# Three adjacency aggregations as 64x64 quadrant products in a four-layer graph network

## Chip, cores and metric

The kernel runs on one core of a Trainium2 chip. The metric is the device time of one execution in microseconds (us). With one core there is no second die to compare with. Engines are named as in the profile: PE is TensorE's matmuls, PEld its weight loads, DVE is VectorE, ACT ScalarE, POOL GpSimd, SP SyncE.

## The reference, cut to what matters

The input x has 128 batches of 64 tokens and 256 channels, in f32. Four layers follow, each `x + layer(relu(layernorm(x)))`. Three products with a 64x64 adjacency matrix concern us:

```python
# layer 0 (A_hat is adj with self loops, normalised by degrees)
agg = jnp.einsum('nm,bmd->bnd', A_hat, features)
h = jax.nn.relu(_batchnorm(agg.reshape(-1, d) @ W1.T + b1, g1, be1))   # statistics over all tokens
...
# layer 1
h = jax.nn.relu(jnp.einsum('ts,bsh->bth', adj, x @ Wg0 + bg0))
h = jax.nn.relu(jnp.einsum('ts,bsh->bth', adj, h @ Wg1 + bg1))
# ... then four small LSTMs over windows of h, which are most of the time
```

Layers 2 and 3 are attentions and are not touched.

## The kernel before

The 8192 tokens are worked on in 16 chunks of 512: four blocks (j) of 128 tokens, each of two batches. An aggregation multiplies each block by a 128x128 matrix with the adjacency twice on its diagonal, so half of each product is with zeros. Channels come in two halves k, and each half has a PSUM bank.

```python
def aggregate(src, mat, name):
    banks = []
    for k in range(KD):                       # KD = 2 channel halves
        ps = bank(f"agg{k}_{name}")           # one of eight PSUM banks, taken in turn
        for j in range(NJ):                   # NJ = 4 blocks of two batches
            nc.tensor.matmul(ps[:, j * P : (j + 1) * P], src[:, j, k * P : (k + 1) * P], mat,
                             start=True, stop=True)
        banks.append(ps)
    return banks
```

Layer 0's first pass, for each chunk c:

```python
xt = l0.tile([P, NJ, D], F32, tag="xt", bufs=3)
nc.sync.dma_start(xt, xr[c])
layernorm_relu(h, xt, f"a{c}")     # bn_stats on DVE, power on POOL, then nmr on DVE, then ACT
agg = l0.tile([P, KD, CH], F32, tag="agg", name=f"agg_{c}")
for k, ps in enumerate(aggregate(h, ahat_t, f"a{c}")):
    nc.vector.tensor_copy(agg[:, k, :], ps)                     # "the copies"
...
for m in range(KH):                                             # 4 output blocks of 128
    ps = bank(f"z1_{c}_{m}")
    for k in range(KD):
        nc.tensor.matmul(ps, w1_sb[:, k, m * P : (m + 1) * P], agg[:, k, :],
                         start=(k == 0), stop=(k == KD - 1))
    nc.scalar.activation(z1[c][m], ps, AF.Identity, bias=bn1_sb[:, 0, m : m + 1])
    nc.vector.bn_stats(st1[:, m, c, :], z1[c][m])               # "the statistics"
```

Within layernorm_relu `rstd` comes from GpSimd:

```python
rsqrt(rstd, mv[:, :, 1], EPS)                        # two POOL instructions
nc.vector.scalar_tensor_tensor(nmr, mv[:, :, 0], -1.0, rstd, op0=OP.mult, op1=OP.mult)   # "nmr"
```

In layer 1, PE's order is written by hand, and the aggregations stand as filler between LSTM steps. In layer 0 no order is written.

## Time and profile before

| What | Value | From |
|---|---|---|
| time | 2206.02 us median of 3 (2201.57 to 2208.31) | timed runs |
| layer 0, first pass: from one chunk's first z product to the next's, from the third chunk on | 9.23 to 9.36 us | PE in order of time |
| start of layer 0's second pass | 177.50 us | the same |
| LSTM stretch, from the first gate product to the last residual transposes | 346.91 to 1747.51, 1400.60 us | the same |
| one aggregation of one chunk in that stretch | 1.78 us | the same, quoted in the prediction |

The last column of such PE lines, in brackets, is idle time just before the group and what ended it; a group's time is best taken from its start to the next group's start, because the ends of pipelined matmuls overlap. The prediction below shows the lines that carry this. DVE in layer 0, in the order in which its instructions were issued (start, duration, line, names):

```profile
127.13 0.66 DVE L237 BATCH_NORM_STATS2 st<-z1b 128x6 f32<-128x512 f32 x1
127.71 1.27 DVE L227 COPY agg<-agg_a 128x512 f32<-128x512 f32 x2
128.90 0.16 DVE L149 SCALAR_TENSOR_TENSOR nmr_a<-mv_a,rstd_a 128x4 f32<-128x4 f32 x1
```

The order is: the last statistics of the previous chunk, the two copies, and then nmr, which belongs to the layernorm of a chunk further on. (Over the whole pass nmr waits 5.0 us for POOL, in four instances.)

### The profile page before, as it was taken

The page shows a single profiled execution, that of the slowest core. Times are in us where ns is not written, and L with a number is a line of the kernel's source. Part 1 is how long each engine was busy: PE and PEld are TensorE (multiplying, and loading weights), DVE is VectorE, ACT ScalarE, POOL GpSimd, SP SyncE. Part 2 cuts the span into 40 slices and gives each one's busy share as a digit, 9 for nine tenths or more (in the row PEclk, how much of TensorE's full clock was granted, in tenths as well). Part 3 has the DMA queues.
Part 4 walks back from the last instruction along what each step waited for, and adds up shares of the span by engine and source line. Part 5 has one row for each costly group of instructions (what it writes and reads, how often), then busy time and mean ns, then how long its engine had stood idle before and what let it go on. Part 6 is the DMA issues. An engine that isn't in the chain of part 4 may idle for free.

```text
span 2205.7 us, 24595 instructions
## 1 busy us (share of the span) xinstructions
PE 2101.8 (95%) x10117; PEld 1339.7 (61%) x10117; DVE 852.5 (39%) x1848; ACT 792.1 (36%) x1433; POOL 168.8 (8%) x216
## 2 busy tenths in 40 slices
PE   6999959999999999999999999999999899999996
PEld 3553435576577468468567657656746756666664
DVE  5643433223323322332332322323222256666664
ACT  3544413233333233333333422333333344444442
POOL 2100010001000000000100100000000011112211
PEclk9999969999999999999999999999999999999998
DMA  3100050000000000000000000000000100000000
GB/s 97 58 20 0 0 186 10 10 1 10 2 9 1 10 10 1 10 10 1 10 10 1 10 10 1 0 0 1 1 0 1 34 11 21 20 21 21 21 20 29
DMA packets 30127, 37.88 MB, mean 17 GB/s; under 512 B 1856, under 2 KB 27456, under 8 KB 30016
## 3 DMA queue, kind: packets, MB, share of 16 engines
q1 hardware_dynamic: 27600, 27.89, 4.1%
q0 software_dynamic: 2256, 8.40, 1.0%
q8 instruction: 79, 1.29, 0.2%
q14 instruction: 32, 0.26, 0.0%
q10 hardware_dynamic: 160, 0.03, 0.0%
HBM read 27.93 MB, written 8.39 MB: 16 GB/s over the span
## 4 chain that ended last, share of the span: by engine, by line
PE 77%; issue 10%; DVE 7%; POOL 3%; DMA 2%; ACT 1%; SPq 0%; POOLq 0%; DVEq 0%; ACTq 0%
PE g L369 32%; PE g L376 17%; PE z L250 5%; PE z L234 3%; PE p_q L500 3%; PE u L340 3%; PE p_k L500 2%; PE v L328 2%; DMA xt<-in_x_dram 2%; PE agg_b L161 1%; PE agg_c L161 1%; PE tr L523 1%; DVE s L514 1%; PE o L643 1%; PE o L588 1%
## 5 line engine op out<-in xcount | busy, mean ns | idle before, releaser
L369 PE MATMUL g<-hT,wih 128*128 128x256 f32 (+2 forms) x2496 | 826.7, 483 | 3.6 <-DVE hT L400 2.7
L369 PEld LDWEIGHTS g<-hT,wih 128*128 128x128 f32 x2496 | 465.0, 188 | 313.1 <-issue 182.4
L382 ACT ACTIVATE gate<-g,bias 128x256 f32<-128x256 f32 (+2 forms) x624 | 350.4, 562 | 820.0 <-PE g L376 648.1
L376 PE MATMUL g<-hs,whh 128*128 128x256 f32 (+2 forms) x1536 | 435.8, 437 | 0.0
L376 PEld LDWEIGHTS g<-hs,whh 128*128 128x128 f32 x1536 | 291.3, 190 | 132.2 <-issue 62.0
L386 DVE TENSOR_TENSOR cell<-cell,gate 128x256 f32<-128x256 f32 (+2 forms) x96 | 48.7, 507 | 449.7 <-ACT gate L382 449.7
L391 DVE TENSOR_TENSOR cell<-gate,gate 128x512 f32<-128x512 f32 (+2 forms) x80 | 48.2, 602 | 213.1 <-ACT gate L382 213.1
L234 PE MATMUL z<-agg,w_sb 128*128 128x512 f32 x256 | 117.5, 613 | 8.6 <-DVE agg L227 7.2
L250 PE MATMUL z<-h,w_sb 128*128 128x512 f32 x256 | 112.1, 601 | 5.0 <-ACT h L245 5.0
L392 ACT ACTIVATE gate<-cell 128x256 f32<-128x256 f32 (+2 forms) x176 | 89.8, 510 | 50.7 <-DVE cell L391 40.3
L410 POOL COPY hn<-hT 128x512 f32<-128x512 f32 x32 | 35.9, 1197 | 784.8 <-DVE hT L400 784.8
L400 DVE TENSOR_TENSOR hT<-gate,gate 128x512 f32<-128x512 f32 (+2 forms) x80 | 48.0, 600 | 114.0 <-PE g L369 96.9
L250 PEld LDWEIGHTS z<-h,w_sb 128*128 128x128 f32 x256 | 49.4, 193 | 67.7 <-issue 57.5
L234 PEld LDWEIGHTS z<-agg,w_sb 128*128 128x128 f32 x256 | 48.6, 195 | 67.4 <-issue 49.0
L395 DVE TENSOR_TENSOR hs<-gate,gate 128x256 f32<-128x256 f32 (+2 forms) x96 | 47.7, 497 | 69.8 <-ACT gate L392 49.6
L385 DVE TENSOR_TENSOR gate<-gate,gate 128x256 f32<-128x256 f32 (+2 forms) x96 | 47.7, 497 | 55.8 <-ACT gate L382 55.8
L508 POOL TENSOR_TENSOR s<-s,mx 128x256 f32<-128x256 f32 (+1 forms) x32 | 40.3, 1259 | 340.3 <-DVE mx L507 251.8
L495 ACT COPY v<-v 128x512 f32<-128x512 f32 x64 | 37.0, 578 | 76.6 <-PE v L492 76.6
L500 PE MATMUL p_q<-hT,w_sb 128*128 128x512 f32 x128 | 61.9, 606 | 0.3 <-DVE hT L175 0.3
L500 PE MATMUL p_k<-hT,w_sb 128*128 128x512 f32 x128 | 60.1, 592 | 0.0
L492 PE MATMUL v<-w_sb,hT 128*128 128x256 f32 x256 | 59.5, 386 | 0.0
L151 ACT ACTIVATE h<-xs,nmr_b,rstd_b 128x256 f32<-128x256 f32 x64 | 34.5, 590 | 69.6 <-DVE nmr_b L149 69.6
(153 smaller groups left out, 2068.1 us busy)
## 6 DMA issues: line engine op xcount, KB each, us to landing
xt<-in_x_dram SPq DMA_DIRECT2D x32, 512.0 KB, 3.8
out_dram<-o SPq DMA_DIRECT2D x16, 512.0 KB, 2.9
wih<-in_wih_t_dram POOLq DMA_DIRECT2D x4, 1024.0 KB, 13.4
whh<-in_whh_t_dram POOLq DMA_DIRECT2D x3, 1024.0 KB, 18.2
w_sb<-in_w_dram SPq DMA_DIRECT2D x1, 768.0 KB, 4.2
wqkv_sb<-in_wqkv_dram SPq DMA_DIRECT2D x1, 768.0 KB, 4.5
w_sb<-in_w1t_dram POOLq DMA_DIRECT2D x1, 512.0 KB, 4.9
w_sb<-in_w2t_dram POOLq DMA_DIRECT2D x1, 512.0 KB, 5.8
```

The lines of the kernel that those rows point to most:

```text
L234: nc.tensor.matmul(ps, w1_sb[:, k, m * P : (m + 1) * P], agg[:, k, :], start=(k == 0), stop=(k == KD - 1))
L250: nc.tensor.matmul(ps, w2_sb[:, k, m * P : (m + 1) * P], h1[:, k, :], start=(k == 0), stop=(k == KH - 1))
L340: nc.tensor.matmul(ps[:, i, :], v[:, k, j * P : (j + 1) * P], wg1_sb[:, k, :], start=(k == 0), stop=(k == KD - 1))
L369: nc.tensor.matmul(banks[q][:, :n].rearrange("p (j w e) -> p j w e", w=nw, e=2), wi[:, k, o], hv[:, k, :, cols, :], start=(k == 0), stop=( ...
L376: nc.tensor.matmul(banks[q][:, :n], wh[:, k, o], hs[:, k, :n], start=False, stop=(k == KD - 1))
L382: nc.scalar.activation(g[q], banks[q][:, :n], AF.Tanh if q == 2 else AF.Sigmoid, bias=bs[:, q * KD + c : q * KD + c + 1])
L386: nc.vector.tensor_mul(cell[c], cell[c], g[1])
L391: nc.vector.tensor_mul(cell[c], g[0], g[2])
L392: nc.scalar.activation(g[2], cell[c], AF.Tanh)
L400: nc.vector.tensor_mul(hv[:, c, :, cols, :], o.rearrange("p (j w e) -> p j w e", w=nw, e=2), t.rearrange("p (j w e) -> p j w e", w=nw, e=2))
L492: nc.tensor.matmul(ps[:, i, :], hT[:, k, j * P : (j + 1) * P], w[:, k, first : first + D], start=(k == 0), stop=(k == KD - 1))
L500: nc.tensor.matmul(ps, w[:, k, m * P : (m + 1) * P], hT[:, k, :], start=(k == 0), stop=(k == KD - 1))
```

## The change

The intent: work only with the two nonzero 64x64 blocks. A product of one batch and 64 channels needs a quarter of the array, and four such products were to run side by side (the prediction reads from layer 3's products that they do), so the aggregation should take less of PE's time.

```diff
 def aggregate(src, mat, name):
-    banks = []
+    banks = [bank(f"agg{e}_{name}").rearrange("p (k j t) -> p k j t", j=NJ, t=T) for e in range(2)]
     for k in range(KD):
-        ps = bank(f"agg{k}_{name}")
         for j in range(NJ):
-            nc.tensor.matmul(ps[:, j * P : (j + 1) * P], src[:, j, k * P : (k + 1) * P], mat,
-                             start=True, stop=True)
-        banks.append(ps)
-    return banks
+            for i in range(2):
+                for e in range(2):
+                    f = slice(k * P + i * T, k * P + (i + 1) * T)
+                    nc.tensor.matmul(banks[e][half(i), k, j, :], src[half(e), j, f],
+                                     mat[half(e), half(e)], start=True, stop=True)
+    return [ps.rearrange("p k j t -> p (k j) t") for ps in banks]
 # layer 0, and alike in layer 1's first aggregation
-for k, ps in enumerate(aggregate(h, ahat_t, f"a{c}")):
-    nc.vector.tensor_copy(agg[:, k, :], ps)
+for e, ps in enumerate(aggregate(h, ahat_t, f"a{c}")):
+    nc.vector.tensor_copy(agg.rearrange("p k (j e t) -> p e (k j) t", e=2, t=T)[:, e], ps)
 # layer 1's second: the interleaved matrix adjt_il goes, ScalarE's ReLU interleaves instead
-for k, ps in enumerate(aggregate(u, adjt_il, f"c{c}")):
-    nc.scalar.activation(hT[:, k, :], ps, AF.Relu)
+for e, ps in enumerate(aggregate(u, adjt_bd, f"c{c}")):
+    nc.scalar.activation(hT.rearrange("p k (n e) -> p e k n", e=2)[:, e],
+                         ps.rearrange("p (k j) t -> p k (j t)", k=KD), AF.Relu)
```

Besides the products, the banks change their meaning: one bank for each parity e of the batch, with both channel halves in it.

More of the change, by code (lines that the diff above doesn't have):

```diff
@@ L152, in layernorm_relu, with half @@
                                  scale=rstd[:, j : j + 1])
+    def half(r):
+        return slice(r * T, (r + 1) * T)
     def aggregate(src, mat, name):
-        banks = []
+        banks = [bank(f"agg{e}_{name}").rearrange("p (k j t) -> p k j t", j=NJ, t=T) for e in range(2)]
         for k in range(KD):
-            ps = bank(f"agg{k}_{name}")
             for j in range(NJ):
-                nc.tensor.matmul(ps[:, j * P : (j + 1) * P], src[:, j, k * P : (k + 1) * P], mat,
-                                 start=True, stop=True)
-            banks.append(ps)
-        return banks
+                for i in range(2):
[4 more added lines that the diff above has]
+        return [ps.rearrange("p k j t -> p (k j) t") for ps in banks]
     def to_channels(dst, src, name):
@@ L225 @@
             agg = l0.tile([P, KD, CH], F32, tag="agg", name=f"agg_{c}")
-            for k, ps in enumerate(aggregate(h, ahat_t, f"a{c}")):
-                nc.vector.tensor_copy(agg[:, k, :], ps)
+            for e, ps in enumerate(aggregate(h, ahat_t, f"a{c}")):
+                nc.vector.tensor_copy(
+                    agg.rearrange("p k (j e t) -> p e (k j) t", e=2, t=T)[:, e], ps)
             lo = res.tile([P, KD, CH], F32, tag=f"r{c}", name=f"z1a_{c}")
@@ L287 @@
         nc.vector.tensor_add(bias, bias, bias2)
-        adjt_il = w1.tile([P, P], F32, name="adjt_il")
-        nc.vector.tensor_copy(adjt_il.rearrange("p (t e) -> p e t", e=2),
-                              adjt_bd.rearrange("p (e t) -> p e t", e=2))
         wih_sb, whh_sb = [], []
@@ L320, in convolutions @@
             agg = l1.tile([P, KD, CH], F32, tag="g", name=f"agg1_{c}", bufs=3)
-            for k, ps in enumerate(aggregate(h, adjt_bd, f"b{c}")):
-                nc.vector.tensor_copy(agg[:, k, :], ps)
+            for e, ps in enumerate(aggregate(h, adjt_bd, f"b{c}")):
+                nc.vector.tensor_copy(
+                    agg.rearrange("p k (j e t) -> p e (k j) t", e=2, t=T)[:, e], ps)
             yield
@@ L535, in columns @@
             return slice(b * T, (b + 1) * T)
-        def half(r):
-            return slice(r * T, (r + 1) * T)
         def pairs(a, r):
```

## The prediction

> **What bounds the kernel now.** I read the page's first line and engine row, then the PE rows by shape, then the table of stretches, then single stretches in order of time.
>
> ```profile
> span 2205.7 us, 24595 instructions
> PE 2101.8 (95%) x10117; PEld 1339.7 (61%) x10117; DVE 852.5 (39%) x1848; ACT 792.1 (36%) x1433; POOL 168.8 (8%) x216
> ...
> L161 PE MATMUL agg_b<-adjt_bd,h 128*128 128x128 f32 x256 | 33.4, 287 | 14.4 <-ACT h L151 14.4
> L161 PE MATMUL agg_a<-ahat_t,h 128*128 128x128 f32 x256 | 33.0, 284 | 1.9 <-ACT h L151 1.9
> L161 PE MATMUL agg_c<-adjt_il,u 128*128 128x128 f32 x256 | 31.0, 275 | 0.0
> ```
>
> TensorE is busy 95% of the span; no other engine passes 39%. The three aggregations hold 97.4 us of it, 4.4%: that is all the change can touch. Each has 16 chunks x 8 products = 128 products and 256 records, so one f32 product is two records, and an aggregation of one chunk is 16 records. Busy is not the same as worth, so I ask in which stretch they lie (columns: window, its length, PE and weight-load busy, clock, DMA share, GB/s; these instructions alone).
>
> ```profile
> 20.00:177.00 157.00, 29.21 (x240) 29.16 (x240) 0.98 0.14 43
> 296.00:347.00 51.00, 9.80 (x64) 9.67 (x64) 0.68 0.48 178
> 347.00:524.00 177.00, 7.86 (x65) 7.76 (x64) 1.00 0.02 6
> 524.00:1590.00 1066.00, 46.70 (x384) 46.57 (x384) 1.00 0.02 5
> ```
>
> So 16 of the 48 blocks lie in layer 0's first pass (up to 177 us), four at the start of layer 1, and 28 inside the LSTM stretch from 347 to 1590 us. In that stretch the same view without the filter shows PE busy 1242.7 of 1243 us: time taken from PE there is time off the kernel. In layer 0 it is otherwise (PE first, then DVE, of one chunk):
>
> ```profile
> 135.41 1.95 PE L161 MATMUL agg_a<-ahat_t,h 128*128 128x128 f32 x16
> 137.67 7.13 PE L234 MATMUL z<-agg,w_sb 128*128 128x512 f32 x16 [0.31 <-DVE agg L227]
> ...
> 136.33 0.69 DVE L237 BATCH_NORM_STATS2 st<-z1b 128x6 f32<-128x512 f32 x1 [1.02 <-ACT z1b L236]
> 136.94 1.27 DVE L227 COPY agg<-agg_a 128x512 f32<-128x512 f32 x2
> ```
>
> The copies out of the aggregation start at 136.94, when DVE is done with the statistics of the previous chunk's last z, which itself waited for ScalarE's evacuation. The first bank was full about 0.9 us after 135.41. So z waits for a chain z, ScalarE, statistics, copy; PE's aggregation lies beside that chain. The reader should see that z began 0.05 us after the first copy (136.94 + 0.68), not after both.
>
> **What the Trainium skill says.** "TensorE: Matmul & The Clock Gate", section "LDWEIGHTS (loading the stationary operand)": loading costs columns / 1.2 ns, whatever the rows. Halving the columns would give 53 in place of 107 ns. The trace's load records are 192 ns for 128 columns and 135 ns for 64: they include latency, so the direction agrees and the formula isn't separately visible. Same page, "Part 3: Packing small matmuls — row/col tiling": matmuls in different row and column groups run concurrently. The trace agrees: 64 records of layer 3's 64x64 products take 1.04 to 1.09 us, 16 to 17 ns each, though each record lasts 218 ns. "TensorEngine Tiling (Array Packing)", "Key Properties": changing the tiling mode drains the engine. The trace shows a small cost, worked out below. Same page, "Gotcha 1: PSUM Pressure": different row tiles have to write different banks. This is why the new banks are one per batch parity e and no longer one per half k of the channels, and that is where I expect the loss.
>
> **The change part by part.** First, PE's work. A block before is 16 records of 128 columns. In the LSTM stretch it costs, from its start to the next group's start, 735.81 - 734.03 = 1.78 us and 776.25 - 774.47 = 1.78 us.
>
> ```profile
> 734.03 1.95 PE L161 MATMUL agg_b<-adjt_bd,h 128*128 128x128 f32 x16
> 735.81 7.37 PE L369 MATMUL g<-hT,wih 128*128 128x512 f32 x16
> ```
>
> A block after is 2 x 4 x 2 x 2 = 32 products, 64 records, of the very shape that layer 3 already has (64-row, 64-column stationary, 64 moving columns, column half outside, row half inside):
>
> ```profile
> 1917.12 1.04 PE L173 MATMUL tc_f<-ident,h 128*128 128x128 f32 x8
> 1918.09 1.16 PE L643 MATMUL o<-v,att 64*64 64x64 f32 x64
> 1919.18 1.98 PE L500 MATMUL p_q<-hT,w_sb 128*128 128x512 f32 x4
> 1921.00 1.88 PE L500 MATMUL p_k<-hT,w_sb 128*128 128x512 f32 x4
> 1922.72 1.88 PE L500 MATMUL p_q<-hT,w_sb 128*128 128x512 f32 x4
> ```
>
> The block itself takes 1.09 us. Going in: the eight transposes before it take 0.97 us to the next start, where eight before an ordinary product take 0.88 (544.77 to 545.65), so 0.09. Coming out: four 512-column records take 1.82, the next four 1.72, so 0.10. Sum 1.28 us, a saving of 0.50 a block. In the LSTM stretch nothing hides it: 28 x 0.50 = 14 us. The arithmetic is a quarter as much, but the time falls only by 28%, because per-record issue and the two changes of mode remain.
>
> Second, the evacuations. Their number and elements stay (two of 512 elements for each block). DVE's writes become runs of 64 elements with gaps; its hT product (L400) writes runs of two elements with gaps and takes 688 ns for 512, against 693 for a plain one (L391), so no dearer. ScalarE's ReLU now writes every second element; no row before shows such a write, and at 36% ScalarE has room even if 598 ns grew. In the LSTM stretch other work lies between the aggregation and its reader (agg_b at 556.76, its v at 572.62), so the new order of copies costs nothing.
>
> Third, in layer 0 nothing lies between. All products now fill both banks to the end of the block, and each bank holds one parity of both channel halves. z's first product needs channel half 0, hence both copies. The block ends about 1.3 us after its start, still before DVE is free (1.53 us after), so copies start where they did, and z starts after the second, 138.21 + 0.05 = 138.26, in place of 137.67: 0.59 later. Given back: today z's second weights wait for the second copy; z's 16 records take 6.97 us where 16 x 0.43 = 6.88 would do, so 0.09. Net loss 0.50 a chunk on 15 chunks (the first z waits for its weights' DMA), 7.5 us. Chunks with a late input load are 0.1 us longer today through two more statistics ahead of DVE's last one; the earlier end of the aggregation frees their buffer sooner, perhaps 0.5 us in all. Loss 7.
>
> Fourth, layer 1's start, two agg_b and two agg_c back to back: agg_b runs from 323.59 to 329.56 at half clock. It is paced by ScalarE until h is complete at about 327; after that half a block and the first v remain, so v might start at 328.1, 1.4 us earlier. agg_c runs 343.34 to 346.91; afterwards the LSTM waits for both ReLUs of the first chunk, to about 345.9, 1.0 earlier. An estimate of 2.4 us. The removed interleaved matrix is one small DVE copy, off the path.
>
> Sum: -14 - 2.4 + 7 = -9.4 us, so 2206.0 - 9.4 = 2196.6, about 2197 us.
>
> **The rivals.** (1) PE is the bound everywhere, so 48 x 0.50 = 24 us come off, 2182 us. For it: 95% busy. Against it: the layer-0 rows above, where the copy ends the wait. It could come about in part if DVE's instructions were ordered anew, with the copies ahead of the last statistics. (2) Changing the mode costs more beside the LSTM's products than in layer 3, or the fourfold number of PE records outruns instruction issue: 0.5 us more a block eats the gain, and with layer 0's loss the kernel becomes 2213. Against it: layer 3 sustains 64 records in 1.09 us amid such changes. (3) The LSTM's recurrence appears as a new wait once the filler is shorter. Against it: after agg_b the next step begins with 16 input products (4.8 to 7.2 us) before it needs hs; agg_c comes after a first-step half whose successor needs no hs. This would cost under 3 us. (4) Bank pressure: two banks at once instead of one after the other. The waits view has no PE wait for the LSTM's banks beyond 0.5 us in total, so I expect nothing.
>
> **Range and chances.** The LSTM part could be 10 to 19 us, layer 0's loss 0 to 9, the start 0 to 4; repeated runs spread from 2201.6 to 2208.3. Not all extremes meet: 2186 to 2205. Faster by over 2% would need 44 us, nearly half of all aggregation time, which a block of 1.28 in place of 1.78 can't give: 0.02. Slower by over 2% would need a mode change near a microsecond: 0.02. Within 2%: 0.96.
>
> **What would show it.** Each aggregation's PE row with 1024 records and 17 to 20 us busy, mean near 220 ns. In the LSTM stretch 1.2 to 1.35 us from an agg block's start to the next group's, and that stretch 14 us shorter. In layer 0 PE's idle time before z for DVE's copies up from 7.2 us to 20 to 26, and a period from z to z up from 9.23 to about 9.7 us. The prediction is wrong if that period is unchanged (DVE reordered), if the block costs 1.7 us or more, or if ScalarE's ReLU grows so much that gates wait for it.

## The result, and the profile after

The changed kernel took 2214.47 us (median of 4, 2213.3 to 2217.57), the kernel before 2206.61 us in its 4 runs. The ratio is 1.0042, with a 95% interval of 1.0022 to 1.0061. All ratios here are the mean time of one kernel's runs over the mean of the other's in the same rounds, so not quite the ratio of the quoted medians. It is within 2%, but slower, by 8 us, where 9 us less was forecast, and outside the range of 2186 to 2205.

First the page of the changed kernel: span, engines, and the aggregations' rows (count, then busy us and mean ns).

```profile
span 2215.7 us, 29204 instructions
PE 2081.9 (94%) x12421; PEld 1301.6 (59%) x12421; DVE 850.8 (38%) x1847; ACT 790.0 (36%) x1433; POOL 168.3 (8%) x216
...
L167 PE MATMUL agg_b<-adjt_bd,h 64*64 64x64 f32 x1024 | 21.0, 233 | 14.7 <-ACT h L151 14.7
L167 PE MATMUL agg_a<-ahat_t,h 64*64 64x64 f32 x1024 | 19.4, 227 | 1.9 <-ACT h L151 1.9
L167 PE MATMUL agg_c<-adjt_bd,u 64*64 64x64 f32 x1024 | 18.4, 221 | 0.0
```

PE was relieved as planned: the aggregations' busy time fell from 97.4 to 58.8 us, and PE's whole busy time by 20 us. Yet the span grew by 10. Such a pair says that PE waits somewhere that it did not. First the place where the gain should be, the LSTM stretch:

```profile
565.23 11.28 PE L373 MATMUL g<-hT,wih 128*128 128x512 f32 x24
576.43 1.16 PE L167 MATMUL agg_b<-adjt_bd,h 64*64 64x64 f32 x64
577.52 7.47 PE L373 MATMUL g<-hT,wih 128*128 128x512 f32 x16
584.83 7.03 PE L380 MATMUL g<-hs,whh 128*128 128x512 f32 x16
```

The block takes 577.52 - 576.43 = 1.09 us. The group ahead of it takes 11.20 where it took 11.11 before (545.65 to 556.76), and the one behind 7.31 where it took 7.20 (558.55 to 565.75). So 1.09 + 0.09 + 0.11 = 1.29 us for the block, against a forecast of 1.28. The whole stretch (368.23 to 1755.07) is 1386.84 us, 13.76 shorter. The gain is there.

The loss is in layer 0. PE's z products of some chunks, in order of time, and the two rows of the table of waits (total us, times, longest) that grew:

```profile
70.21 7.14 PE L240 MATMUL z<-agg,w_sb 128*128 128x512 f32 x16 [2.34 <-DVE agg L232]
...
80.78 7.13 PE L240 MATMUL z<-agg,w_sb 128*128 128x512 f32 x16 [2.34 <-DVE agg L232]
...
92.14 8.83 PE L240 MATMUL z<-agg,w_sb 128*128 128x512 f32 x16 [3.14 <-DVE agg L232]
...
158.19 7.13 PE L240 MATMUL z<-agg,w_sb 128*128 128x512 f32 x16 [1.60 <-DVE agg L232]
...
168.02 7.13 PE L240 MATMUL z<-agg,w_sb 128*128 128x512 f32 x16 [1.60 <-DVE agg L232]
```

```profile
PE z L240 <- DVE agg L232: 35.6, 15, 5.0
...
DVE nmr_a L149 <- POOL rstd_a L81: 20.6, 14, 1.5
```

The second pass starts at 199.80 in place of 177.50 us: 22.3 us lost, where 7 were forecast. The last four intervals are 9.83 us, 0.60 above the 9.23 of before; the forecast was about 9.7. The eleven before them are 10.56 us or longer. And nmr now waits 20.6 us for POOL, where the same row of before has 5.0. The chain of waits shows it in its place (start, us, what):

```profile
76.47 0.61 DVE st L243
77.08 0.16 DVE mv_a L145 x2
77.28 0.11 issue
77.39 0.24 POOL rstd_a L80
77.62 0.07 issue
77.70 1.05 POOL rstd_a L81
78.77 0.16 DVE nmr_a L149
78.93 0.60 DVE st L243
79.53 1.20 DVE agg L232 x2
80.78 7.15 PE z L240 x16
```

Read from below: z waited for both copies, the copies stood behind the last statistics, these stood behind nmr, and nmr waited for POOL's power. No data go from nmr to these statistics or copies; nmr is for a later chunk. It merely stands ahead of them in DVE's order, which the compiler had changed. The Trainium skill's "PSUM — Partial Sum Buffer", section "Engine vs sequencer instructions", says that VectorE's queue is strictly first in, first out; this trace agrees, as DVE sat idle for 1.54 us ahead of nmr (77.23 to 78.77) while the statistics' input was ready from 78.07 (ScalarE, 77.38 + 0.69).

The last four intervals have no such wait because no layernorm is left to prepare. They therefore separate the terms: 0.60 us a chunk for the second copy, 10.57 - 9.83 = 0.74 us for the wait. In two further chunks z itself ran 8.83 in place of 7.13 us. In the first the granted clock over 92.14 to 100.90 is 0.81 (0.50 from 92.71 to 96.12), after PE had idled 3.14 us; in the other it is 0.81 too, after 2.34 us. I call these z products at half clock, though the clock is halved for only a part of them.

What is left of the 10 us in the spans: from the second pass's start to layer 1's first aggregation another 1.0 us went (the shift grows from 22.3 to 23.3); layer 1's start, from agg_b to the first gate product, is 1.95 us shorter (23.32 to 21.37; forecast 2.4). The part after the LSTMs, which the change does not touch, is 460.6 in place of 458.2 us in these two profiles; in the other profiles it lies between 456.8 and 461, and I draw nothing from it: one and the same kernel has 456.8 in the eighth run and 460.7 in the tenth. The four profiles without quadrants in layer 1 all have 458.1 to 458.2; why the others scatter is not known.

### The profile page after: what moved, and what is told of

It is laid out like the page before. It is cut to its first block, busy times and chain, and to the rows that moved or that the text cites. A ratio compares the mean times of both kernels' runs of the same rounds, so it can differ in the third digit from the quotient of the medians. Undisturbed runs are those within 1.5% of the kernel's fastest.

```text
span 2215.7 us, 29204 instructions
## 1 busy us (share of the span) xinstructions
PE 2081.9 (94%) x12421; PEld 1301.6 (59%) x12421; DVE 850.8 (38%) x1847; ACT 790.0 (36%) x1433; POOL 168.3 (8%) x216
## 4 chain that ended last, share of the span: by engine, by line
PE 76%; issue 10%; DVE 8%; POOL 3%; DMA 2%; ACT 1%; SPq 0%; POOLq 0%; DVEq 0%; ACTq 0%
PE g L373 32%; PE g L380 17%; PE z L256 5%; PE z L240 4%; PE p_q L504 3%; PE v L331 2%; PE u L343 2%; PE p_k L504 2%; DMA xt<-in_x_dram 2%; PE tr L527 1%; DVE st L243 1%; PE agg_b L167 1%; PE o L644 1%; DVE s L518 1%; PE o L589 1%
## 5 line engine op out<-in xcount | busy, mean ns | idle before, releaser
L240 PE MATMUL z<-agg,w_sb 128*128 128x512 f32 x256 | 122.5, 634 | 37.8 <-DVE agg L232 35.6
```

## The experiments

**Theory A**: the quadrants do what was forecast; layer 0 loses because of the banks. z needs both copies, and the compiled order of DVE puts a wait for POOL ahead of them. **Rival B**: quadrant products amid full-array products delay layer 0 by themselves. Later rivals stand with their runs. An overview (medians in us; "period" is from z to z from the third chunk on, "pass 2" the start of layer 0's second pass, "LSTM" the length of that stretch, all from the profiles):

| Kernel | us | ratio to before | period | pass 2 | LSTM |
|---|---|---|---|---|---|
| before | 2205 to 2207 | 1 | 9.23 to 9.36 | 177.50 | 1400.60 |
| changed | 2214.47 | 1.0042 | 10.56 to 12.27, last four 9.83 | 199.80 | 1386.84 |
| 1 changed, order mended | 2198.25 | 0.9972 | 9.83 | 185.72 | 1386.83 |
| 2 quadrants in layer 1 only | 2191.14 | 0.993 | 9.23 to 9.33 | 175.69 | 1386.83 |
| 3 quadrants in layer 0 only | 2230.98 | 1.0116 | 10.56 to 12.26, last four 9.83 | 199.45 | 1400.58 |
| 4 before, banks alone changed | 2230.82 | 1.0117 | 10.88 to 12.57, last four 9.85 | 199.51 | 1400.59 |
| 5 as 2, copies first | 2188.9 | 0.993 | 8.80 to 9.23 | 171.98 | 1386.84 |
| 6 as 1, copies first | 2198.3 | 0.9969 | 9.62 | 182.23 | 1386.83 |
| 7 as 1, four banks | 2194.92 | 0.9955 | 9.36 | 178.59 | 1386.84 |
| 8 as 7, copies first | 2186.23 | 0.9909 | 8.68 to 8.88 | 167.78 | 1386.83 |
| 9 before, order alone changed | 2220.77 | 1.0068 | 10.49 to 12.19, last three 9.23 | 194.61 | 1400.58 |

The LSTM column alone says that layer 1's part is settled: 13.76 us wherever the quadrants are in layer 1, nothing where they are not.

**1. The changed kernel with DVE's order mended.** One edge of order for each chunk, no wait, no other work:

```diff
-nc.vector.scalar_tensor_tensor(nmr, mv[:, :, 0], -1.0, rstd, op0=OP.mult, op1=OP.mult)
+with tc.issue_after(behind) if behind is not None else nullcontext():   # behind: the second copy of chunk c-4
+    nc.vector.scalar_tensor_tensor(nmr, mv[:, :, 0], -1.0, rstd, op0=OP.mult, op1=OP.mult)
```

> The changed kernel, with one order edge for each chunk of layer 0: VectorE's small product for a later chunk's layernorm (which waits for GpSimd's power) is issued behind the two copies out of the aggregation, as in the kernel before, where the changed kernel issues it ahead of the last statistics and the copies. Theory A (the lost 22 us of layer 0 are the second copy, 0.60 us a chunk, plus this wait, 0.74 us a chunk and more in the first chunks, plus clock drops that the longer idle brings): z-to-z periods of 9.8 us where the changed kernel has 10.57, no half-clock z in mid-stage, PE's idle before z down from 35.6 to about 24 us, and 2203 to 2206 us. Rival B (the quadrant products and their mode changes delay layer 0 by themselves): the period stays near 10.6 and the time at 2214.

Measured: 2198.25 us (2197.62 to 2201.48), ratio 0.9972 (0.9957 to 0.9987). DVE, and z behind it:

```profile
122.51 0.69 DVE L244 BATCH_NORM_STATS2 st<-z1b 128x6 f32<-128x512 f32 x1 [0.88 <-ACT z1b L243]
...
123.12 1.27 DVE L233 COPY agg<-agg_a 128x512 f32<-128x512 f32 x2
124.31 0.15 DVE L150 SCALAR_TENSOR_TENSOR nmr_a<-mv_a,rstd_a 128x4 f32<-128x4 f32 x1
124.45 7.13 PE L241 MATMUL z<-agg,w_sb 128*128 128x512 f32 x16 [1.60 <-DVE agg L233]
```

The period is 9.83 us from the third chunk to the last, no z from the third chunk on runs at half clock, and PE's idle time before z for DVE is 25.8 in place of 35.6 us. The same products and banks, 16 us less by the medians (which are of different rounds): theory A holds, and B cannot explain it. The expected 2203 to 2206 us were missed on the good side: the order's share had been set too low, for layer 0 got back 14.1 of its 22.3 us (199.80 to 185.72). Idle time came out at 25.8 for an expected 24 us. This is also the kernel that the prediction had described, and its 2197 us are met within 2.

**2. Quadrants in layer 1 only.** Layer 0 calls the aggregate of the kernel before (kept as `aggregate_bd`, with its copies); layer 1 is as changed.

```diff
-for e, ps in enumerate(aggregate(h, ahat_t, f"a{c}")):
-    nc.vector.tensor_copy(agg.rearrange("p k (j e t) -> p e (k j) t", e=2, t=T)[:, e], ps)
+for k, ps in enumerate(aggregate_bd(h, ahat_t, f"a{c}")):
+    nc.vector.tensor_copy(agg[:, k, :], ps)
```

> Quadrant products in layer 1's two aggregations alone; layer 0 keeps its block-diagonal products, banks and copies. Theory A: layer 0 exactly as before (periods of 9.23 to 9.34), the LSTM stretch shorter by 13.8 us (28 blocks by 0.49) and layer 1's start by 2, so 2190 to 2193 us. Rival B: the quadrants cost wherever other matmuls stand around them, so that less than 8 us are gained and the time is over 2198.

Measured: 2191.14 us, ratio 0.993 (0.9913 to 0.9946). Periods as before, the LSTM stretch 13.77 us shorter. As theory A has it.

**3. Quadrants in layer 0 only.** The reverse: layer 0 as changed, layer 1 with `aggregate_bd` and its interleaved matrix.

```diff
-for k, ps in enumerate(aggregate(u, adjt_il, f"c{c}")):      # the kernel before
+for k, ps in enumerate(aggregate_bd(u, adjt_il, f"c{c}")):   # layer 0 alone calls the quadrant aggregate
```

> Quadrant products in layer 0's aggregation alone; layer 1 as before. Theory A and B both: layer 0 as in the changed kernel, 20 to 24 us longer, and nothing gained later: 2226 to 2231 us. If the parts don't add up (under 2222 or over 2234), something couples the layers.

Measured: 2230.98 us, ratio 1.0116 (1.0101 to 1.0131). The parts nearly add up: about +25.7 here and -14.2 in the second run make +11.5, against +8 for the whole; the 3.5 us between them are less than the 4.3 us over which the changed kernel's own four runs lie. Layer 0 is the same in both profiles: the second pass starts at 199.45 here and at 199.80 there, and two z products from the third chunk on run at half clock in each.

**4. The kernel before with other banks.** No quadrant; the two banks are split by half of the tokens, so that z needs both copies, as in the changed kernel.

```diff
-for k, ps in enumerate(aggregate(h, ahat_t, f"a{c}")):
-    nc.vector.tensor_copy(agg[:, k, :], ps)
+for g, ps in enumerate(aggregate_j(h, ahat_t, f"a{c}")):   # banks[j // 2][:, k, j % 2, :]
+    nc.vector.tensor_copy(agg.rearrange("p k (g r) -> p g k r", g=2)[:, g], ps)
```

> The kernel before, with its block-diagonal products, but in layer 0 the two banks are split by half of the tokens in place of half of the channels, so that z's first product needs both copies, as it does in the changed kernel; no quadrant anywhere. Its compiled VectorE order shows the small layernorm product ahead of the last statistics too. Theory A: layer 0 loses about as much as in the changed kernel, 17 to 24 us, periods of 10.3 to 10.7, so 2223 to 2231 us. Rival B: with no quadrant product there is no loss, 2205 to 2210 us.

Measured: 2230.82 us, ratio 1.0117 (1.0102 to 1.0132), the same loss as with quadrants in layer 0. Two chunks of it, one with nmr and one of the last four:

```profile
100.75 0.16 DVE L149 SCALAR_TENSOR_TENSOR nmr_a<-mv_a,rstd_a 128x4 f32<-128x4 f32 x1 [1.54 <-POOL rstd_a L81]
100.83 0.69 DVE L245 BATCH_NORM_STATS2 st<-z1b 128x6 f32<-128x512 f32 x1
101.44 1.27 DVE L235 COPY agg<-agg_a 128x512 f32<-128x512 f32 x2
...
102.76 7.13 PE L242 MATMUL z<-agg,w_sb 128*128 128x512 f32 x16 [1.96 <-DVE agg L235]
...
167.67 7.13 PE L242 MATMUL z<-agg,w_sb 128*128 128x512 f32 x16 [0.93 <-DVE agg L235]
```

The total is the same as in the third run, its parts are not quite: periods of 10.88 us (above the expected 10.3 to 10.7) against 10.56, and three half-clock z products against two. In the last four chunks, where no nmr is left, z starts 2.88 us after the block's start in place of 2.26: that is the second copy's cost with no quadrant product in sight.

So the way the banks are split is enough to make the compiler put nmr ahead, and enough to lose layer 0's time. Rival B falls. Why the scheduler decides so was not examined.

**5. As the second, with the copies ahead of the last statistics.** The statistics of chunk c-1's fourth block are emitted behind the copies of chunk c:

```diff
-    nc.vector.bn_stats(st1[:, m, c, :], z1[c][m])
+    if m < KH - 1:
+        nc.vector.bn_stats(st1[:, m, c, :], z1[c][m])
 # after the copies of chunk c
+if c:
+    with tc.issue_after(copied[c]):
+        nc.vector.bn_stats(st1[:, KH - 1, c - 1, :], z1[c - 1][KH - 1])
```

nmr stands behind the copies as in the first run.

> Layer 1 in quadrants, layer 0 block-diagonal as in the kernel before (the second experiment), and in layer 0 VectorE's order is changed: the copies of chunk c are issued ahead of the last statistics of chunk c-1. Theory A (in layer 0 the copies wait behind those statistics, not for PE): z starts when the first bank is full and copied, about 1.85 us after the aggregation's start, in place of 2.26; periods of 8.7 to 8.8 us in place of 9.23 to 9.34, so 6 to 8 us less than the second experiment: 2183 to 2185 us. Rival C (PE's block-diagonal products set z's start): no change, 2191.

Measured: 2188.9 us, ratio 0.993 (0.9913 to 0.9946). The mechanism is there (z 1.84 us after the block's start, 122.61 to 124.45, and periods of 8.8 in most chunks), but the expected 6 to 8 us are missed: the second pass begins 3.7 us earlier than in the second run, and the medians differ by 2.2. Periods with an input load are 9.0 to 9.2, and in this profile one more early z ran at half clock. By the ratios the two kernels cannot be told apart (0.993 both). The rival of this expectation, C, falls all the same: PE's products did not change, and the period did.

**6. As the first, with the copies ahead of the last statistics.** The same edit on the first run's kernel.

> The changed kernel with its order mended (the first experiment) and with the copies ahead of the last statistics too. Theory A: both copies can start only when the whole block is done, 1.3 us after its start, and z needs both, so z starts at 2.65 in place of 2.76 us: periods of 9.7, 2195 to 2198 us. So reordering helps the quadrants little as long as z needs both copies.

Measured: 2198.3 us, ratio 0.9969 (0.9954 to 0.9984), periods of 9.62. The time is 0.3 us above the expected range. As expected, the order helps little while z needs both copies and both banks fill to the end.

**7. As the first, with four half-filled banks**, one for each channel half and parity, the channel half outermost, and four copies of 256 elements:

```diff
+def aggregate_k(src, mat, name):
+    for k in range(KD):
+        banks = [bank(f"agg{e}{k}_{name}")[:, : CH // 2].rearrange("p (j t) -> p j t", t=T) for e in range(2)]
+        ...                                  # products as changed, for this k only
+        for e in range(2):
+            yield k, e, banks[e]
+for k, e, ps in aggregate_k(h, ahat_t, f"a{c}"):
+    copied[c] = nc.vector.tensor_copy(agg[:, k, :].rearrange("p (j e t) -> p e j t", e=2, t=T)[:, e], ps).ins
```

> The first experiment with four half-filled banks in layer 0, one per channel half and parity, and the channel half outermost: quadrant products, but z's first product needs only the first two copies of 256 elements. Theory A: the 0.6 us for the second copy shrink to about 0.1; periods of 9.25 to 9.4, 2189 to 2193 us, no better than the second experiment although layer 0's aggregation is 28% shorter. Rival C (the quadrants' mode changes cost layer 0 its time): stays at 9.8, 2198.

Measured: 2194.92 us (2191.61 to 2195.39), ratio 0.9955 (0.9938 to 0.9971). The period of 9.36 is as expected, so this run's rival C (the changes of mode cost layer 0 its time, 9.8 us) falls; the time is 2 us above the expected range. The point stands: even without the wait for a second whole copy, shorter products alone do not beat the second run, which leaves layer 0 as it was.

**8. Both: four banks, and the copies ahead of the last statistics.**

> The kernel just named with the copies ahead of the last statistics. Theory A: the copies start when the first channel half is done, 0.8 us after the block's start, z at about 1.6 us; only here does layer 0 profit from the quadrants: periods of 8.5 to 8.8, 2179 to 2184 us, the fastest of all.

Measured: 2186.23 us (2180.58 to 2186.69), ratio 0.9909 (0.9893 to 0.9925), the fastest, though its median is 2 us above the expected range. z starts 1.65 us after the block, as worked out:

```profile
127.98 1.16 PE L180 MATMUL agg_a<-ahat_t,h 64*64 64x64 f32 x64
...
128.72 1.41 DVE L246 COPY agg<-agg_a 128x256 f32<-128x256 f32 x4 [0.94 <-PE agg_a L180]
...
129.63 4.96 PE L257 MATMUL z<-agg,w_sb 128*128 128x512 f32 x11 [0.49 <-DVE agg L246]
```

With the copies ahead of the statistics they wait for PE's aggregation, as they did in the fifth and sixth runs (0.19 to 1.20 and 1.24 us of DVE's idle time in the chunks I looked at). Here, where z needs only the first half of the shorter products, their being short counts in layer 0: periods of 8.68 to 8.88 against 8.80 to 9.23 in the fifth run.

**9. The kernel before in all but the order.** Banks, copies and products of before; an edge of order puts the last statistics of chunk c-5 behind nmr of chunk c. Rival D was that the order hurts only where z needs both copies.

```diff
+if c >= 5:   # NoSync: order only
+    tc.add_manual_dep(last_stat[c - 5], small_product.name,
+                      mybir.DependencyInfo(mybir.DependencyClass.NoSync, mybir.DependencyReason.DATA), reason="order")
```

> The kernel before in all but one order edge: in layer 0 VectorE issues the last statistics of chunk c-5 behind the small layernorm product of chunk c, which waits for GpSimd; banks, copies and products stay. Theory A: the wait alone costs what it cost in the fourth experiment, where z's idle time was 1.96 us with it and 0.94 without: 1.0 us in each of some 11 chunks, 11 us, plus up to two half-clock z of 1.7 us: 2216 to 2221 us. Rival D (the order matters only because z needs both copies): under 2210.

Measured: 2220.77 us, ratio 1.0068 (1.0055 to 1.0082): 15 us from the order of one small DVE instruction. One chunk of it, and the z of the next:

```profile
97.92 0.16 DVE L149 SCALAR_TENSOR_TENSOR nmr_a<-mv_a,rstd_a 128x4 f32<-128x4 f32 x1 [1.54 <-POOL rstd_a L81]
98.01 0.69 DVE L244 BATCH_NORM_STATS2 st<-z1b 128x6 f32<-128x512 f32 x1
98.61 1.27 DVE L234 COPY agg<-agg_a 128x512 f32<-128x512 f32 x2
...
99.34 8.83 PE L241 MATMUL z<-agg,w_sb 128*128 128x512 f32 x16 [2.55 <-DVE agg L234]
...
111.53 7.13 PE L241 MATMUL z<-agg,w_sb 128*128 128x512 f32 x16 [1.58 <-DVE agg L234]
```

The period is mostly 10.49 us while layernorms are left (idle time before z 1.58 in place of 0.31) and 9.23 in the last three. Three half-clock z products from the third chunk on are part of the 15 us. Rival D falls.

**10 and 11. The eighth and the second again, side by side, with more rounds.**

> The eighth experiment's kernel again, for a closer interval beside the next: 2181 to 2187 us.

> The second experiment's kernel again, on the same chip as the run before: 2187 to 2192 us, 4 to 6 us behind it, because layer 0's periods are 9.23 to 9.33 here and 8.68 to 8.88 there.

Measured: 2184.71 us, ratio 0.99 (0.9885 to 0.9915), and 2189.45 us, ratio 0.9925 (0.9913 to 0.9938). Their intervals overlap slightly in these rounds, but the order of the two is that of runs 8 and 2, and the profiles show where it comes from (second pass at 167.78 against 175.69). The version with quadrants everywhere, four banks and mended order beats the kernel before by about 1%.

## Why the prediction was wrong

**Right.** PE's saving for each block was forecast as 0.50 us and measured as 0.49 or so; 28 blocks were to give 14 us and gave 13.76, to within 0.02 us in every profile with quadrants in layer 1. Layer 1's start gave 1.95 for a forecast 2.4. That the LSTM's recurrence and the PSUM banks would add no wait holds too. ScalarE's strided ReLU went from 598 to 627 ns; gates did not wait for it, and only layer 1's start shows a new wait of 0.3 us. That layer 0 would lose and not gain, and that the second copy is why, was right in kind and nearly in size: 0.60 for a forecast 0.50 us a chunk, 9.0 of the 22.3 us lost. The difference is the 0.09 us that the forecast gave back inside z: z's 16 records still take 6.97 us to the next group's start in the last four chunks of the fourth run, though both copies are there before it begins. The first experiment, with the order as it had been assumed, gives layer 0 a loss of 8.2 us (177.50 to 185.72) for a forecast 7, and 2198.25 us for a forecast 2197. Rival 2 of the prediction names 2213 us, close to the 2214 measured, but that is luck: it rests on a dearer block, and the block takes 1.29 us as forecast.

**Wrong.** The step that failed is in the third part, on layer 0: "The block ends about 1.3 us after its start, still before DVE is free (1.53 us after), so copies start where they did". They did not: they start 2.18 us after the block's start (77.27 to 79.45), because DVE was free later, not because of PE. Layer 0 lost 22.3 us, where the range allowed 0 to 9. The step took DVE's order of before as given. It is compiled anew with every change, and here the small product that waits for POOL moved ahead of the copies. I had thought of a new order only as a gain, in the first rival ("if DVE's instructions were ordered anew, with the copies ahead of the last statistics"). The ninth run shows that such a move alone can cost 15 us, the fourth that the change of banks alone brings it about.

**The 22.3 us of layer 0 in the changed kernel**, from the intervals between z starts: 15 x 0.60 = 9.0 for the second copy; 11 x 0.74 = 8.1 for the wait on POOL; 2 x 1.70 = 3.4 for z products at half clock (8.83 - 7.13); the remaining 2.6 of the 23.1 us lie in the first two intervals and in the one from 80.78 to 92.14, where the same wait met an input load and, at the start, a longer stretch at half clock (the second z took 10.07 us, before 8.83). The first z started 0.7 us earlier, which leaves 22.3. The clock drops follow from the longer idle time, as far as traces alone can show it. In each trace here the granted clock changes only on a grid of periods of 3.41 us. I went through the periods that began at full clock in all 13 profiles, from 40 us to 10 us before the second pass: in ten of them PE idled 0.56 to 0.83 of the period, and the next was granted 0.50; in the other 473 it idled 0.54 or less, and none was followed by a drop. So a gap of 2.34 us costs clock only where enough of it falls into one period: in the changed kernel PE idled 61% of 123.44 to 126.85, and the clock fell; it idled 52% of 113.20 to 116.61, and it did not. A gap of 1.60 us, 47% of a period, is too short, and all ten drops are in kernels where nmr stood ahead (runs 3, 4, 9 and the changed kernel). No experiment moved the gaps on purpose, and in the first chunks one period of the eighth run idled 0.58 without a drop.

## What to carry to other kernels

Before you count on an engine being free at the same moment as before, ask whether its order is yours or the compiler's; after a change of buffers or banks, compare the compiled orders of every engine, since one small instruction that waits for a slow engine can hold up everything behind it. When you re-split accumulation banks, split them along the axis in which the consumer reads, or its first product will wait for the last copy. And read what a saving on the busiest engine is worth stage by stage: here it was worth all of its 14 us in one stage, and nothing in another as long as DVE's chain set the pace there.

## What the Trainium skill lacked or had wrong

- "TensorEngine Tiling (Array Packing)", section "Key Properties", says that a change of tiling mode drains the engine, with no cost. Here the group of 128x128 products ahead of a 64x64 block took 0.09 us longer, and the one behind it 0.10 to 0.11.
- "TensorE: Matmul & The Clock Gate", section "Wait — 56ns, not 53.3ns?", gives about 25 ns as a floor from one matmul's start to the next, and names no exception there. 64 quadrant records of 64 columns took 1.09 us, 17 ns each: the sentence does not hold for products that take turns over four quadrants, which the page's own part on packing, named in the prediction, lets run concurrently.
- The same page, section "Why this matters for your kernels", asks for no PE gaps over about 3 us. Here the granted clock fell to 0.80 over a z of 8.83 us (124.52 to 133.18 in the fourth run) after a gap of 1.96 us in a chunk that had no longer one. Three of ten such gaps in that run were followed by a drop; after gaps of 1.60 in the first run it stayed at 1.00. What told them apart was PE's idle share of a 3.41 us period, 0.56 and more against 0.54 and less.
- No page that I read gives a time for a ScalarE write with a step of two elements; what is said of steps in SBUF is general. Here it is 627 against 598 ns for 512 f32 elements.
